# Where a small transpose stands in a step, and three more steps without expert work, in an attention and mixture-of-experts kernel

## Chip, core and metric

The kernel runs on one core of a Trainium2 chip. The metric is the device time of one execution in microseconds. Three executions of the kernel before took 560.89, 562.18 and 559.4 us; their median is 560.89 us.

## What is computed

The input is x with 8 batches of 512 tokens of 128 values, in float32. Each token is normalised (layer norm without weights). The result is x plus an attention block plus a feed-forward block, both fed with the normalised tokens:

```python
xn = _layernorm(x, axis=-1)
x = x + _L0_attn_ref(xn, W1, b1, Wp, bp) + _L0_ffn_ref(xn, gate_w, expert_gate, ...)
...
# attention: 16 heads of 8 dimensions, causal
w = jnp.einsum('bhqd,bhkd->bhqk', q, k) / dk
w = jax.nn.softmax(w * mask - (1.0 - mask) * NEG_BIG, axis=-1)
a = jnp.einsum('bhqk,bhkd->bhqd', w, v)
...
# feed-forward: one shared expert, and the 2 best of 8 routed experts for each token
silu(x @ gw.T) * (x @ uw.T) @ dw.T      # gw, uw: 352x128, dw: 128x352
```

## The kernel before

**Engines and names.** PE is TensorE (matmuls; PEld are its weight loads), DVE is VectorE, ACT is ScalarE, POOL is GpSimd, SP is SyncE, which issues most DMAs. The order of instructions on PE, DVE, ACT and SP is written out by hand: each engine runs its queue in the order in which the Python code issues it. What the code below calls a step is one pass of the inner loop at the end of the function.

**Attention steps.** For each batch there are four groups of four heads, so there are 32 groups (n), and each has five score tiles (i = 0 to 4). That makes 160 steps, step = 5n + i, with a run-in of AHEAD = 9 steps numbered -9 to -1. A step does the following, in this order:

1. `weigh`: PE computes a tile of transposed scores (`fill`, L339) into the PSUM tile scT, which has one buffer, and ACT takes the exponential (L467). The causal mask comes either from extra matmuls (L324) or, from step BUSY = 22 on and as long as not all expert results are placed (`len(placed) < NB`), from POOL (L474).
2. Rows of expert results that are ready are scattered to DRAM by POOL (`to_place`, L679), and row shifts that are ready are written by SP (`puts`, L451).
3. `look(step + 9)`: the softmax needs the maximum of every row before its scores are used. Nine steps ahead PE computes scores in the other orientation (`peak_scores`, L383) into the PSUM tile sc, which also has one buffer, and DVE takes maxima over them (L412, L417, L421, L422). After the fifth tile of a group, `shift_parts` (L427, L432, L433, three small DVE operations) makes the negated maxima, split in two parts.
4. `extra()`: one chunk of expert work, unless the step is in the set `alone`. A chunk (`chunk`) is PE's L664, ACT's tanh (L669) and DVE's L670 and L672. A block of the expert stream has three chunks; along with them come entries for the list `aside`: two `down` groups of the block before (PE's L697, followed by ACT's L704 for a routed block or DVE's L708 for a shared one) and `turn_slots` for a block to come (L638). The stream has 52 blocks: 13 of the shared expert, 36 routed and 3 shared ones at the end. After the last chunk one more call issues the last two `down` groups.
5. `prepare`: ACT copies a mask into the next sc tile (L371) for tiles 0 and 2, once routing is done.
6. `some_routing`: one piece of the routing of tokens to experts, mostly on DVE, up to step 24 (L1042 to L1163).
7. `side`: what is due in this step (the list `ready`), then two entries of `aside`.
8. The weighted sums of earlier tiles (`attend`, L491), and things due `behind` all else (projections L264 and L284, the output projection L579 with its addition to x by DVE, L584). A group pair's sums are turned by L542 (`divide`, three steps after the pair), a batch's by L563 (`turn`).

**The row shift.** The split maxima of a group (128 rows by 32 columns) are transposed by PE (`shift`, L439) into a PSUM tile, DVE copies that to SBUF (L443), and SP writes it as two extra rows of the query operand (`put_shift`, L451), so that the fill adds the negated maximum to each score. In the kernel before, `look` for the fifth tile makes the shift due in the next step, in point 7 of the list above: it is issued behind that step's chunk. That next step is always one with i = 1, step 5n - 4 for group n. SP's two writes are issued at the start of the step after that, and the fills that need them begin at step 5n.

**PSUM buffers.** The tile of the transposed maxima, the chunk's result (gu), the down group's result (y), the turned tokens (s_ps), projections and turned sums all share three rotating PSUM buffers (`misc`). Each new tile takes the buffer of the one issued three places before it and waits until that has been read.

**Steps without expert work.** Steps 3, 5, ..., 19 and 12, 16 and 20 make up the set `alone`, in the stretch in which routing runs. Seven calls come before the run-in and nine in it. The last chunk is issued in step 151 and the last `down` groups in step 152, so steps 153 to 159 have no expert work.

**The end.** When all expert results are in DRAM, POOL adds them to x by 16 gathering DMAs (L732), in the order first places of batches 0 to 5, second places of batches 0 to 5, then first places of batches 6 and 7, then second places of 6 and 7. Those of batches 6 and 7 come after the shared expert's rows for these batches have been added (L708). The last group's sums are then turned and projected, and L584 adds them to x for the last batch. SP and ACT write the output (L1299).

Of the kernel before, what the change touches and what calls it, by code (L numbers as in the profile page):

```python
# [35 lines left out]
AHEAD = 9  # L36
# [17 lines left out]
PIECE = 8  # L54
FILL = 2
BUSY = 22
PLACES = TOPK * NT * P
EPS = 1e-5
MASKED = -1e30
# [8 lines left out]
def attn_moe_kernel(  # L68
# [59 lines left out]
    for i in range(NV):  # L128
        t = const.tile([P, NC, H, 32], F32, name=f"v_ext{i}")
# [71 lines left out]
    for i in range(2):  # L201
        t = const.tile([P, NF, PAIR], F32, name=f"h{i}")
# [17 lines left out]
    table = dram1.tile([NT * P, ROW], F32, name="table")  # L220
    results = dram1.tile([PLACES, E], F32, name="results")

# [71 lines left out]
    def fetch(u, i0=0, i1=HP):  # L294

        from_q, from_k = in_dram[divmod(u, 2)]
        for t in range(2):
            heads = slice(t + 2 * i0, min(t + 2 * i1, HH), 2)
            for a in range(2):
                at_ = SIDE * t + 2 * D * a  # L300
                nc.sync.dma_start(
                    ks[at_ : at_ + 2 * D, u % NU, i0:i1].bitcast(F32),
                    from_k[:, :, heads].rearrange("r d h s -> (r d) h s"),
                )
                if a == 0:
                    nc.sync.dma_start(
                        qs[at_ : at_ + 2 * D, u % NU, i0:i1].bitcast(F32),
                        from_q[:, :, heads].rearrange("r d h s -> (r d) h s"),
                    )
                else:  # L310
                    for r in range(2):
                        nc.sync.dma_start(
                            qs[at_ + D * r : at_ + D * r + D, u % NU, i0:i1].bitcast(F32),
                            from_q[1 - r, :, heads],
                        )
# [92 lines left out]
    def maxima(n, i):  # L408

        ps = peak_scores(n, i)  # L410
        if i == 4:
            nc.vector.tensor_reduce(  # L412
                tops[:, :, :, 2],
                ps.rearrange("p t (u k) -> p t u k", u=2), AX.X, ALU.max,
            )
        elif i in MASKED_TILES:
            nc.vector.tensor_reduce(  # L417
                diag[:, :, i // 2, :], ps.rearrange("p t (b k) -> p t b k", k=P), AX.X, ALU.max
            )
        else:  # L420
            nc.vector.tensor_reduce(tops[:, :, i // 2, 3], ps[:, :, : 3 * P], AX.X, ALU.max)  # L421
            nc.vector.tensor_reduce(tops[:, :, i // 2, 1], ps[:, :, 3 * P :], AX.X, ALU.max)  # L422

    def shift_parts(n):

        top = at.tile([P, 2, 2 * NC], F32, name="row_max")
        nc.vector.tensor_tensor(  # L427
            top.rearrange("p t (i c) -> p t i c", c=NC), tops, diag, ALU.max
        )
        parts = at.tile([P, 2, 2, 2 * NC], F32R, name="m_parts")  # L430
        hi, lo = parts[:, :, 0], parts[:, :, 1]
        nc.vector.tensor_scalar_mul(hi, top, -1.0)  # L432
        nc.vector.scalar_tensor_tensor(lo, top, -1.0, hi.bitcast(F32), ALU.mult, ALU.subtract)  # L433
        return parts
# [28 lines left out]
    def weigh(n, kind, j, by_pool, spare):  # L463

        ps = fill(n, kind, j, by_pool, spare)
        pT = pr.tile([P, 2, S], F32, name="pT")
        nc.scalar.activation(pT, ps, AF.Exp, scale=D**-0.5)  # L467
        if by_pool:
            if kind == "half":
                diagonals = [pT.rearrange("p t (u k) -> p (t u) k", u=2)[:, :, :P]]  # L470
            else:
                diagonals = [pT[:, :, :P]] + ([pT[:, :, 3 * P :]] if kind == "mixed" else [])
            for d in diagonals:
                m = nc.gpsimd.affine_select(  # L474
                    out=d, in_=d, pattern=[[0, d.shape[1]], [1, P]], compare_op=ALU.is_ge,
                    fill=0.0, base=0, channel_multiplier=-1,
                )
                masked.append(m.ins)
        return pT
# [197 lines left out]
    def place_rows(at_, o):  # L677
        with on_pool():
            d = nc.gpsimd.indirect_dma_start(  # L679
                results, bass.IndirectOffsetOnAxis(ap=goal[:, at_ : at_ + 1], axis=0), o, None,  # L680
                bounds_check=PLACES - 1, oob_is_err=False,
            )
# [70 lines left out]
    def due(step, f, to=None):  # L753
        (ready if to is None else to).setdefault(step, []).append(f)

    def look(t):
        n, i = divmod(t, NTILES)
        maxima(n, i)
        if i == NTILES - 1:
            return lambda: due(t - AHEAD + 1, partial(shift, n, shift_parts(n)))  # L760
        return lambda: None

    def side(step, most):

        for f in ready.pop(step, []):
            then(step, f())
        for _ in range(most):
            if aside:
                aside.pop(0)()

    def behind(step):

        for f in behind_all.pop(step, []):
            then(step, f())
# [8 lines left out]
    def extra():  # L783
        do, more = next(beside, (None, []))
        if do is None and not more:
            through.append(True)
        if do is not None:
            do()
        aside.extend(more)
# [129 lines left out]
    def route():  # L919
# [235 lines left out]
        absent = ro.tile([P, NB], F32, name="absent")  # L1155
        nc.vector.tensor_scalar(absent, turn_, 0.5, float(PLACES + S + P), ALU.is_lt, ALU.mult)
        nc.vector.scalar_tensor_tensor(goal, number, -float(P), absent, ALU.add, ALU.add)
# [10 lines left out]
    def some_routing():  # L1168
        if not done_routing and next(routing, "end") == "end":
            done_routing.append(True)  # L1170
            early.close()
            later_pools["wexp"] = pool("wexp", 3 * MB)
            later_pools["inp"] = pool("inp", 6)
            later_pools["turned"] = pool("turned", 3)
            later_pools["scales"] = pool("scales", 4)
# [46 lines left out]
        due(first + (1 if b < 3 else 2), partial(project_qk, b, 1), behind_all)  # L1222
        due(at_ + (8 if b > 1 else 3), partial(project_v, b), behind_all)
    routed = -2
    alone = set(range(3, 21, 2)) | {12, 16, 20}
    for t in range(AHEAD):
        while puts:
            puts.pop(0)()
        parts_then = look(t)
        extra()  # L1230
        parts_then()
        if t - AHEAD >= routed:
            some_routing()
        side(t - AHEAD, 2)
        behind(t - AHEAD)
    for n in range(B * NG):
        b, g = divmod(n, NG)
        waiting = []
        for i, (kind, j) in enumerate(TILES):
            step = n * NTILES + i  # L1240
            if i == 1 and n % 2 == 1 and (n + 3) // 2 < 2 * B:
                fetch((n + 3) // 2)
            by_pool = step >= BUSY and len(placed) < NB
            spare = step >= total_steps - AHEAD + 1 and step % 2 == 1
            waiting.append((kind, j, weigh(n, kind, j, by_pool, spare)))
            while to_place:
                to_place.pop(0)()
            while puts:
                puts.pop(0)()
            parts_then = look(step + AHEAD) if step + AHEAD < total_steps else lambda: None  # L1250
            if step not in alone:
                extra()
            parts_then()
            if done_routing and step + AHEAD + 1 < total_steps:
                prepare(*divmod(step + AHEAD + 1, NTILES))
            if step >= routed:
                some_routing()
            side(step, 2)
            for f in late:
                f()  # L1260
            behind(step)
            late = []
            if i == NTILES - 1 and n == B * NG - 1:
                evacuate(n, av, halves[0])
            if i == 1 and g % 2 == 0:
                av = av_ps.tile([P, S], F32, name="av")
            if i in (1, 4) or (i == 3 and n == B * NG - 1):
                late = [partial(attend, n, waiting, av)]
                waiting = []
            if len(placed) == NB:  # L1270
                for _ in range(2):
                    if to_gather and (to_gather[0][1] < kept or through):
                        gather(*to_gather.pop(0))
        if n == B * NG - 1:
            break
        if g % 2 == 1:
            late.append(partial(evacuate, n, av))
            due(step + 3, partial(divide, n))
        if g == NG - 1:
            due(step + 4, partial(turn, b))  # L1280
            due(step + 5, partial(join, b), behind_all)
# [78 lines left out]
```

## Time and profile before

| What | Value |
|---|---|
| median of three executions | 560.89 us |
| the profiled execution's own time | 561.91 us |
| its span, first to last instruction | 559.9 us |
| mean granted TensorE clock | 0.988 |
| all transposes of maxima (L439) | 32, 0.27 us each, weight load 0.10 |
| their copies by DVE (L443) | 32, 0.27 us each |
| step 0 begins, step 22, step 28 | 52.20, 129.99, 150.50 us |
| step 152 begins, step 153, step 156 | 536.16, 540.02, 543.93 us |

The profile is of one execution. Times are in microseconds from the first instruction. In a line of instructions the columns are start, duration, engine, line, operation, what it writes and reads, sizes and count, and in brackets the idle time of the engine before it with what ended it. Matmuls overlap, and their ends are modelled, so the start of the next instruction says more than a duration. A profile's stretch runs from one given time to another, and shows each engine's busy time in it.

### The profile page before, as it was taken

What the parts mean: (1) busy time and instruction counts of PE and PEld (TensorE: products, weight loads), DVE (VectorE), ACT (ScalarE), POOL (GpSimd) and SP (SyncE); (2) the same over time, 40 slices, a digit from 0 to 9 for tenths busy, and PEclk for the clock granted to TensorE, in tenths of its full rate; (3) what the DMA queues carried; (4) which work ended last, traced back from release to release, by engine and by line L of the source; (5) the groups of instructions that cost most, each with busy time, mean ns of one, the idle gap of its engine ahead of it and who ended that gap; (6) DMA issues with size and microseconds to landing.
All of it is one profiled execution on the core that took longest, in us unless ns stands there. A gap on an engine that the chain in (4) does not pass through costs nothing.

```text
span 559.9 us, 12488 instructions
## 1 busy us (share of the span) xinstructions
PE 530.1 (95%) x4492; PEld 380.5 (68%) x4492; DVE 433.5 (77%) x1057; ACT 353.5 (63%) x566; POOL 260.5 (47%) x439
## 2 busy tenths in 40 slices
PE   4899989889999999999999999999999999999995
PEld 2676655556676777767776777767767777877753
DVE  5878998999877777877787787868688778877731
ACT  4453544564566766877677766867667766777652
POOL 8630020001343556656656556656655766443710
PEclk9999998899999999999999999999999999999997
DMA  6651251816318583584629575674919677640993
GB/s 212 152 75 22 72 83 60 132 51 128 68 39 148 147 156 105 133 207 131 120 87 166 162 165 144 120 167 128 161 45 195 180 164 199 154 110 4 158 207 90
DMA packets 34050, 70.66 MB, mean 126 GB/s; under 512 B 6980, under 2 KB 9288, under 8 KB 33990
## 3 DMA queue, kind: packets, MB, share of 16 engines
q1 hardware_dynamic: 26278, 56.47, 43.8%
q0 software_dynamic: 6848, 13.13, 12.0%
q8 instruction: 36, 0.59, 0.5%
q10 hardware_dynamic: 864, 0.27, 0.2%
q14 instruction: 24, 0.20, 0.2%
HBM read 52.31 MB, written 17.27 MB: 124 GB/s over the span
## 4 chain that ended last, share of the span: by engine, by line
PE 76%; DVE 18%; ACT 2%; issue 2%; DMA 1%; POOL 0%; DVEq 0%; ACTq 0%
PE gu L664 24%; PE av L491 12%; PE y L697 11%; PE scT L339 9%; PE sc L383 9%; DVE diag L417 3%; PE qk_ps L264 3%; DVE tops L421 2%; DVE there L1080 2%; PE p_ps L579 1%; DVE h L672 1%; DVE th L670 1%; PE ot L542 1%; PE s_ps L638 1%; DVE parts L266 1%
## 5 line engine op out<-in xcount | busy, mean ns | idle before, releaser
L467 ACT ACTIVATE pT<-scT 128x1024 f32<-128x1024 f32 x156 | 160.0, 1026 | 63.7 <-PE scT L339 28.1
L474 POOL TENSOR_SCALAR_AFFINE_SELECT pT<-pT 128x256 f32<-128x256 f32 (+1 forms) x173 | 73.7, 440 | 182.3 <-ACT pT L467 179.4
L664 PE MATMUL gu<-sT,w 128*128 128x256 f32 (+1 forms) x480 | 121.2, 379 | 0.3 <-DVE h L672 0.3
L417 DVE TENSOR_REDUCE diag<-sc 128x8 f32<-128x1024 f32 x64 | 78.1, 1221 | 45.9 <-PE sc L383 33.8
L669 ACT ACTIVATE th<-gu 128x256 f32<-128x256 f32 (+1 forms) x156 | 59.6, 382 | 64.8 <-PE gu L664 61.0
L383 PE MATMUL sc<-ks,qs 33*128 33x128 f32 (+3 forms) x896 | 82.0, 283 | 10.0 <-DVE tops L422 4.5
L664 PEld LDWEIGHTS gu<-sT,w 128*128 128x128 f32 x480 | 76.2, 189 | 17.0 <-DVE h L672 0.5
L491 PE MATMUL av<-pT,v_ext 128*32 128x512 f32 (+3 forms) x1024 | 82.6, 440 | 1.8 <-ACT pT L467 1.3
L670 DVE SCALAR_TENSOR_TENSOR th<-th,gu 128x256 f32<-128x256 f32 (+1 forms) x156 | 64.6, 414 | 21.5 <-ACT th L669 18.3
L339 PE MATMUL scT<-qs,ks 35*128 35x512 f32 (+3 forms) x498 | 78.5, 372 | 1.2 <-ACT pT L467 1.2
L679 POOL DMA_INDIRECT results<-o,goal x71 | 72.3, 1018 | 15.8 <-issue 15.8
L383 PEld LDWEIGHTS sc<-ks,qs 33*128 33x128 f32 (+1 forms) x896 | 66.5, 186 | 18.6 <-DVE diag L417 4.9
L623 POOL DMA_INDIRECT s<-table,token x71 | 69.2, 974 | 20.7 <-issue 15.3
L339 PEld LDWEIGHTS scT<-qs,ks 35*128 35x128 f32 x498 | 39.5, 184 | 56.3 <-issue 26.1
L672 DVE TENSOR_TENSOR h<-gu,th 128x256 f32<-128x256 f32 (+1 forms) x156 | 65.6, 421 | 5.4
L421 DVE TENSOR_REDUCE tops<-sc 128x2 f32<-128x768 f32 x64 | 60.8, 950 | 2.5 <-PE sc L383 1.4
L697 PE MATMUL y<-w,h 128*128 128x128 f32 x426 | 59.2, 275 | 0.3 <-DVE parts L266 0.3
L697 PEld LDWEIGHTS y<-w,h 128*128 128x128 f32 x426 | 56.2, 192 | 4.1 <-DVE parts L266 0.7
L371 ACT CAST sc<-mask_q 128x1024 f32<-128x1024 bf16 x50 | 50.9, 1018 | 6.9 <-DVE tops L422 4.8
L664 PE MATMUL gu<-xnT,ws_sb 128*128 128x256 f32 x192 | 54.7, 411 | 0.0
L491 PEld LDWEIGHTS av<-pT,v_ext 128*32 128x32 f32 x1024 | 25.3, 109 | 23.8 <-issue 14.6
L664 PEld LDWEIGHTS gu<-xnT,ws_sb 128*128 128x128 f32 x192 | 33.5, 193 | 10.9 <-issue 3.8
(209 smaller groups left out, 584.3 us busy)
## 6 DMA issues: line engine op xcount, KB each, us to landing
w<-in_w_exp_dram SPq DMA_DIRECT2D x40, 576.0 KB
ks<-dk SPq DMA_DIRECT2D x60, 128.0 KB
dq<-parts SPq DMA_DIRECT2D x16, 256.0 KB
dk<-parts SPq DMA_DIRECT2D x16, 256.0 KB
qs<-dq SPq DMA_DIRECT2D x64, 64.0 KB
x_sb<-results POOLq DMA_DIRECT2D x16, 256.0 KB
qs<-dq SPq DMA_DIRECT2D x30, 128.0 KB
table<-rows SPq DMA_DIRECT2D x4, 520.0 KB
```

The costliest lines, as they stand in the source:

```text
L339: nc.tensor.matmul(out_, lhsT=k[:, ts(i, P)], rhs=q[:, i * P :], start=first, stop=True, skip_group_check=True,)
L383: nc.tensor.matmul(ps[:, jj % 2, ts(at_, P) if count == 1 else ds(at_ * P, count * P)], lhsT=q[:, ts(c, P)], rhs=k[:, key * P : (key + cou ...
L417: nc.vector.tensor_reduce(diag[:, :, i // 2, :], ps.rearrange("p t (b k) -> p t b k", k=P), AX.X, ALU.max)
L421: nc.vector.tensor_reduce(tops[:, :, i // 2, 3], ps[:, :, : 3 * P], AX.X, ALU.max)
L467: nc.scalar.activation(pT, ps, AF.Exp, scale=D**-0.5)
L474: m = nc.gpsimd.affine_select(out=d, in_=d, pattern=[[0, d.shape[1]], [1, P]], compare_op=ALU.is_ge, fill=0.0, base=0, channel_multiplier=-1,)
L491: nc.tensor.matmul(av[32 * jj : 32 * jj + 32, c * P :], lhsT=v_ext[b % NV][:, c, at_, :], rhs=weights, start=(c == 0 and g % 2 == 0), stop ...
L664: nc.tensor.matmul(gu[:, i, part], lhsT=w[c][:, ds(i * FP + f * P, P)], rhs=sT[:, part], start=True, stop=True,)
L670: nc.vector.scalar_tensor_tensor(th, th, 1.0, gu[:, 0], ALU.add, ALU.mult)
L672: nc.vector.tensor_tensor(h[own_, f, :slots], gu[own_, 1], th[own_], ALU.mult)
L679: d = nc.gpsimd.indirect_dma_start(results, bass.IndirectOffsetOnAxis(ap=goal[:, at_ : at_ + 1], axis=0), o, None, bounds_check=PLACES - 1 ...
L697: nc.tensor.matmul(y, lhsT=h[:, f, ts(c, P)], rhs=w[c % len(w)][:, ds(2 * FP + f * P, P)], start=(f == 0), stop=(f == NF - 1),)
```

## The change

There are two edits. First, a transposed shift is no longer put into the list of things due in the next step, but into a list of its own, `shifts`. That list is emptied in the next step right behind the scores and ahead of the chunk from step SOON = 25 on, and behind the chunk, but ahead of `prepare` and routing, before that. Second, steps 22, 24 and 26 join the set `alone`, so they issue no chunk. The number of chunks stays the same; the calls that these steps would have made are made by later ones.

```diff
+SOON = 25
...
+    shifts = []
+
+    def turn_shifts(when):
+        while shifts and when:
+            shifts.pop(0)()
+
     def look(t):
         n, i = divmod(t, NTILES)
         maxima(n, i)
         if i == NTILES - 1:
-            return lambda: due(t - AHEAD + 1, partial(shift, n, shift_parts(n)))
+            return lambda: shifts.append(partial(shift, n, shift_parts(n)))
         return lambda: None
...
-    alone = set(range(3, 21, 2)) | {12, 16, 20}
+    alone = set(range(3, 21, 2)) | {12, 16, 20, 22, 24, 26}
     for t in range(AHEAD):
         while puts:
             puts.pop(0)()
         parts_then = look(t)
         extra()
+        turn_shifts(True)
         parts_then()
...
             parts_then = look(step + AHEAD) if step + AHEAD < total_steps else lambda: None
+            turn_shifts(step >= SOON)
             if step not in alone:
                 extra()
+            turn_shifts(step < SOON)
             parts_then()
```

## The prediction

> **What bounds the kernel now.** I read the page first, then the waits of PE, then each engine's timeline. I number a step by its transposed-score fill (L339), which opens it on PE; there are 160, and the first starts at 52.20 us.
>
> ```profile
> PE 530.1 (95%) x4492; PEld 380.5 (68%) x4492; DVE 433.5 (77%) x1057; ACT 353.5 (63%) x566; POOL 260.5 (47%) x439
> ...
> PEclk9999998899999999999999999999999999999997
> ```
>
> PE is busy nearly everywhere. The clock is short of full in two early slices and in the last one. The waits of PE say how little idle time there is to win:
>
> ```profile
> PE sc L383 <- DVE tops L422: 4.5, 7, 1.2
> PE sc L383 <- DVE diag L417: 3.1, 4, 1.4
> ...
> PE gu L664 <- DVE h L672: 0.3, 1, 0.3
> ```
>
> Columns: total us, times, longest. Scores (L383) wait for DVE's maxima, because the score tile has one PSUM buffer. In the timeline nearly all of these waits lie before step 22, where routing loads DVE. Only one expert matmul group (L664) ever waits, for 0.3 us. After step 27 the steps are PE back to back, so a step costs what its matmuls cost. The six steps that the change strips and their neighbours (22 to 27), a stretch each:
>
> ```profile
> 129.99:133.20 3.21, 3.21 (x25) 1.92 (x24) 2.93 (x10) 1.41 (x2) 0.77 (x2) 1.00 0.20 69
> 133.20:136.70 3.50, 3.50 (x34) 2.79 (x31) 3.33 (x10) 1.97 (x3) 0.77 (x2) 1.00 0.75 130
> 136.70:140.00 3.30, 3.30 (x27) 2.94 (x26) 3.16 (x11) 1.43 (x3) 0.64 (x1) 1.00 0.90 124
> 140.00:143.17 3.17, 3.17 (x36) 1.81 (x35) 3.03 (x11) 1.41 (x2) 0.41 (x1) 1.00 0.55 62
> 143.17:147.06 3.89, 2.93 (x26) 2.23 (x23) 3.02 (x8) 2.35 (x3) 0.92 (x2) 1.00 0.01 1
> 147.06:150.50 3.44, 3.44 (x27) 2.24 (x26) 3.21 (x9) 2.39 (x3) 2.48 (x4) 1.00 0.20 44
> ```
>
> Columns: length, then busy us of PE, PEld, DVE, ACT, POOL, then clock. PE is full except for 0.96 us in step 26, but DVE is nearly full too: 18.68 of 20.51 us. So work taken off PE here soon meets DVE.
>
> **Prices.** Step 12 goes from scores (93.04) to weighted sums (94.06) over the L542 turns in 1.02 us; step 22 has a chunk between and takes from 130.34 to 132.21, 1.87. One chunk costs PE 0.85. Steps 134 and 139 differ by the six matmuls of L697, 2.43 against 1.76: 0.67. On DVE a chunk is two operations, start to start 0.45 and 0.40, and each L697 group one of 0.28.
>
> **Part 1, transposes from step 25 on.** Nothing is added: 26 transposes (L439), their DVE copies (L443) and two small DMAs each move forward within their step. Step 26 has no chunk to pass, so 25 really move. The transpose issues in 0.11 us (161.37 to 161.48) before or after the chunk alike. It needs the split maxima of L433, which end 0.4 to 1.8 us before the chunk starts (381.12 against 381.54 in the tightest, step 101), so PE should not wait there; if it did, the chunk and all PE work would queue behind it. DVE's copy, 0.27, now goes between the diagonal maxima and the tanh product. In step 136 the maxima end at 493.17 and ACT's tanh at 493.35, so 0.18 of the copy fills a hole. On SP the writes stay where they are, popped at the next step's start; they are only ready some 1 us sooner. They were issued at 495.0 for a fill at 500.94, so no fill gains. One true gain: the three small PSUM buffers rotate, and the next step's chunk now reuses the buffer that the copy frees, not the one that L672 frees. That removes the single 0.26 us wait (step 37). Before step 25 the move passes only routing and prepared masks: same DVE sum, nothing. Bounds for part 1: -0.5 (twice the visible wait) to +1.3 (25 times 0.05, half an issue slot); I take -0.26, the row itself.
>
> **Part 2, the stripped steps.** The three missing calls delay all later expert work by three calls, exactly one block of three chunks. The pattern of chunk against step, period three, is thus unchanged. By step 28, 3 chunks and 2 down groups have left PE: 3 x 0.85 + 2 x 0.67 = 3.9 us. I walk the queues by the rows:
> - Step 22: 2.36 instead of 3.21. DVE ends its maxima at 132.12, then does routing (1.24), divide (0.8), and starts step 23's maxima at 134.1, before at 135.12.
> - Steps 23 and 24 shrink to 2.83 and 1.78 on PE, which reaches step 25 at about 137.0. DVE still owes a chunk (0.85), routing of L1147 to L1153 (1.2) and step 24's maxima (1.2), ending near 138.5. Step 25's scores wait there about 1.4 us.
> - Step 26: the scores wait 0.2 for ACT's mask copy and go at 142.4 (before 144.63). Step 27: PE waits 0.5 for maxima that end at 144.3; its scores go at 144.4, before at 147.40.
>
> Gain at step 28: about 2.9, since some 2 us of new waits replace the old 0.96. It is carried to the end. A second gain: the last routed result is placed three steps later, so steps 145 to 147 keep POOL's masks and drop PE's (L324). Steps 146 and 126 have equal matmuls but for these, 2.86 against 2.67; three such steps give about 0.5.
>
> **What comes back.** The same 3.9 us return in steps 152 to 155, where there were two down groups at 152 and then no expert work. What can swallow them is this idle time:
>
> ```profile
> 541.94 0.50 PE L339 MATMUL sc<-qs,ks 35*128 35x512 f32 x2 [0.65 <-ACT pT L467]
> ...
> 545.74 1.07 PE L491 MATMUL av<-pT,v_ext 128*32 128x512 f32 x8 [0.65 <-ACT pT L467]
> ...
> 548.66 1.07 PE L491 MATMUL av<-pT,v_ext 128*32 128x384 f32 x16 [0.65 <-ACT pT L467]
> ```
>
> Only the first wait (step 155) has the returned chunks before it; it goes. The others follow fills without expert work and stay. Against it, the last down groups need the last chunk's hidden tile. In step 151 that tile ended 3.0 us after the step's start (534.35 to 537.37), ACT's exponential going first. Step 154 is only about 1.5 us long, so step 155 waits about 0.6 for it; before, the turns of L542 covered most of this. Returned: 3.9 - 0.65 + 0.6 - 0.24 (the old wait of step 152) = 3.6.
>
> **Sum.** -2.9 - 0.5 - 0.26 + 3.6 = -0.1 us on a profiled time of 561.91 (span 559.9 and 2.0 around it). The profiled run is 1.0 above the median, 560.89, so I forecast 560.8.
>
> **The clock.** This view of four stretches shows a price that the sum leaves out:
>
> ```profile
> 82.24:85.65 3.41, 2.52 (x30) 1.76 (x29) 3.36 (x9) 1.67 (x3) 0.21 (x1) 1.00 0.00 0
> 85.65:89.07 3.42, 3.42 (x14) 2.44 (x17) 2.33 (x7) 0.81 (x2) 0.00 (x0) 0.50 0.00 0
> 95.89:99.31 3.42, 2.05 (x29) 1.20 (x25) 3.38 (x11) 2.70 (x3) 0.00 (x0) 1.00 1.01 345
> 99.31:102.72 3.41, 3.41 (x14) 2.37 (x14) 3.38 (x14) 1.04 (x2) 0.00 (x0) 0.50 1.07 132
> ```
>
> Twice a stretch in which PE ran almost only score matmuls of 33 to 64 rows, 2.0 to 2.5 us of them, was followed by 3.41 us at half clock. Step 10 took 5.79 us there, against 3.84 for its like (step 45). [...] By the rows a busy but thin stretch is enough, and the sum would be +1.6. I follow the rows, as a rival.
>
> **Rivals.**
> 1. *DVE keeps up* (0.20). If routing's small operations overlap more than I walk, the 2 us of waits vanish: -0.1 - 2.0 = -2.1, 558.8; with the 0.6 of step 155 gone too, 558.2. For it: DVE has only 18.68 of 20.51 us. Against: DVE ran without a gap over 0.2 us from 130.65 to 144.8, and its order is fixed.
> 2. *Slower: the clock halves in steps 24 to 28* (0.17). Between step 25's weighted sums (to 142.0) and step 27's chunk (144.8) PE has 2.8 us of thin work, where 81.5 to 85.41 tripped it. It decides if a clock window of 3.41 us falls onto this gap with under about 0.5 us of full-height matmuls in it. Price 1.7 each: 562.5, and twice, 564.2.
> 3. *The last gather ends last* (0.08). The last expert row update moves from 539.42 to about 542.8, and POOL's last gathers hang on it:
>
> ```profile
> 539.75 1.76 POOL L732 DMA_DIRECT2D x_sb<-results  x2 [7.22 <-DMA x_sb<-results]
> 547.32 0.87 POOL L732 DMA_DIRECT2D x_sb<-results  x1 [5.81 <-DMA x_sb<-results]
> ```
>
> SP saw that last one landed at 551.58; the final addition (L584) starts at 555.69. A slack of 4.1 against a delay of 3.4 leaves 0.7. Slower transfers by 2 us would give +1.3, 562.1.
>
> **Chances.** Forecast 0.55, rivals 0.20, 0.17, 0.08. A measurement tells about 0.5%, 2.8 us. Over that faster takes the longer half of rival 1 and a little beyond: 0.15. Over that slower takes most of rival 2 doubled, or with 3: 0.18. Within: 0.67. The range takes in rival 1's 558.2 and rival 2's 564.2.
>
> **What would show it.** Right: scores of step 25 waiting over 1 us for L422; step 26's wait for the mask copy shrinking to 0.2; step 28 near 147.6 and step 152 near 532.5; L664 with no wait on L672; no L324 in steps 145 to 147; step 156 within 0.5 us of 543.93. Wrong: no wait at step 25 (rival 1), clock 0.50 between 135 and 150 (rival 2), L584 waiting for the gather (rival 3), or transposes that wait for L433.

## The result and the profile after

The changed kernel took 566.11 us (median of 6 runs, 564.53 to 569.33), the kernel before, on the same chip, 561.16 us (6 runs, 559.4 to 562.18). The ratio is 1.0089, with a 95% interval of 1.0068 to 1.0110: slower by 5.0 us, where -0.1 was forecast, and above the range. The profiled execution of the changed kernel took 564.53 us, with a span of 562.3, against 561.91 and 559.9.

From here on a line number of the changed kernel is one higher than before, up to the edited loop (L339 is L340, L664 is L665, L732 is L733). The page after:

```profile
PE 528.7 (94%) x4476; PEld 380.2 (68%) x4476; DVE 434.1 (77%) x1057; ACT 353.9 (63%) x566; POOL 262.2 (47%) x443
...
PEclk9999999999899999999999999999999999999997
```

Next to the page of before nothing stands out: the busy times differ by 1.7 us or less, and the clock row has one 8 where it had two. The change has to be read stage by stage. I cut both profiled executions at the same steps:

| Stretch | before, us | after, us | difference |
|---|---|---|---|
| up to step 22 | 129.99 | 128.12 | -1.87 |
| steps 22 to 27 | 20.52 | 21.40 | +0.88 |
| steps 28 to 151 | 385.65 | 383.07 | -2.57 |
| steps 152 to 155 | 7.77 | 11.95 | +4.18 |
| step 156 to the end | 15.96 | 17.74 | +1.78 |

Most of the first row isn't the change: step 10 took 5.79 us before, under the half clock that starts at 85.65, and 4.18 after, where the profiled execution had none. The stripped steps, a stretch for each of 22 to 27, with the columns as in the prediction (the last two are the busy share of the DMA engines and GB/s):

```profile
128.12:130.42 2.30, 2.30 (x22) 1.16 (x22) 2.23 (x8) 1.02 (x1) 0.66 (x2) 1.00 0.33 108
130.42:133.24 2.82, 2.82 (x28) 2.07 (x25) 2.68 (x8) 1.35 (x2) 0.88 (x3) 1.00 0.83 150
133.24:135.21 1.97, 1.97 (x18) 1.56 (x17) 1.83 (x8) 1.58 (x3) 0.27 (x1) 1.00 0.76 111
135.21:142.49 7.28, 5.70 (x41) 3.54 (x40) 6.06 (x18) 2.42 (x3) 0.78 (x2) 0.77 0.42 54
142.49:144.19 1.70, 1.12 (x15) 0.81 (x11) 0.69 (x1) 1.02 (x1) 0.00 (x0) 1.00 0.00 0
144.19:149.51 5.32, 5.23 (x26) 3.46 (x26) 3.13 (x7) 2.32 (x3) 1.18 (x3) 0.68 0.01 3
```

Steps 22 to 24 and 26 shrink about as walked. Steps 25 and 27 swell from 3.17 to 7.28 and from 3.44 to 5.32. The new waits and the clock (0.77 and 0.68) share this: in the kernel with FIRST = 12 below, at full clock, the same two steps take 5.67 and 3.76. The same time cut into stretches of 3.41 us at the clock's own changes:

```profile
134.90:138.32 3.42, 1.84 (x13) 1.26 (x12) 3.25 (x13) 1.02 (x1) 1.06 (x2) 1.00 0.76 106
138.32:141.73 3.41, 3.41 (x17) 2.13 (x19) 3.09 (x8) 1.40 (x2) 0.00 (x0) 0.50 0.24 25
141.73:145.15 3.42, 2.75 (x39) 1.74 (x31) 1.41 (x2) 1.44 (x2) 0.41 (x1) 1.00 0.00 0
145.15:148.56 3.41, 3.41 (x18) 2.74 (x17) 2.05 (x4) 1.82 (x3) 0.77 (x2) 0.50 0.02 5
```

The halved stretches are the second and the fourth; each follows a window in which PE was busy 1.84 or 2.75 of 3.41 us. The new wait lies in the first of these windows. PE's timeline in step 25 (start, duration, instruction, idle time before it):

```profile
135.21 0.50 PE L340 MATMUL scT<-qs,ks 35*128 35x512 f32 x2
137.28 0.50 PE L384 MATMUL sc<-ks,qs 33*128 33x256 f32 x4 [1.58 <-DVE tops L423]
137.72 1.53 PE L665 MATMUL gu<-xnT,ws_sb 128*128 128x256 f32 x4
```

The wait is the forecast one (1.4 forecast, 1.58 measured), and the chunk behind it takes 1.53 instead of 1.13 at the lower clock.

The four steps in which the work comes back, first of the kernel before, then of the changed one:

```profile
536.16:543.93 7.77, 7.09 (x90) 4.46 (x90) 2.42 (x8) 4.18 (x5) 1.76 (x2) 1.00 0.77 196
```

```profile
532.59:544.53 11.94, 11.75 (x114) 8.23 (x114) 5.10 (x15) 5.48 (x8) 3.98 (x5) 1.00 1.12 213
```

PE's busy time grows by 4.66 and its idle time falls from 0.68 to 0.19. Last, the end. POOL's timeline holds the last scatter of routed results and the gathers, DVE's the final addition. First the kernel before (its last gather is in the prediction), then the changed one:

```profile
515.46 1.00 POOL L679 DMA_INDIRECT results<-o,goal  x1 [0.16 <-issue]
518.35 6.38 POOL L732 DMA_DIRECT2D x_sb<-results  x7 [1.90 <-DMA results<-o,goal]
```

```profile
555.69 0.42 DVE L584 TENSOR_TENSOR x_sb<-p_ps,x_sb 128x256 f32<-128x256 f32 x1 [2.53 <-PE p_ps L579]
556.54 0.42 DVE L584 TENSOR_TENSOR x_sb<-p_ps,x_sb 128x256 f32<-128x256 f32 x1 [0.43 <-PE p_ps L579]
```

```profile
521.62 1.00 POOL L680 DMA_INDIRECT results<-o,goal  x1 [0.15 <-issue]
524.52 7.28 POOL L733 DMA_DIRECT2D x_sb<-results  x8 [1.90 <-DMA results<-o,goal]
...
546.81 1.76 POOL L733 DMA_DIRECT2D x_sb<-results  x2 [9.00 <-DMA x_sb<-results]
554.52 0.87 POOL L733 DMA_DIRECT2D x_sb<-results  x1 [5.95 <-DMA x_sb<-results]
```

```profile
558.55 0.76 DVE L585 TENSOR_TENSOR x_sb<-p_ps,x_sb 128x256 f32<-128x256 f32 x2 [4.80 <-DMA x_sb<-results]
```

Before, the addition waited for p_ps, PE's output projection of the last batch; now it waits for the last gather. PE began p_ps at 554.77 (554.43 before), and before, the addition came 1.26 after that. So it could have come at about 556.0 and comes 2.5 later. The kernel's end is delayed by less: before, the second half of the addition waited another 0.43 for p_ps, and now both halves run together. From the start of p_ps to the end it is 7.50 instead of 5.46, so the late gather costs 2.0 in this execution.

### The profile page after: what moved, and what is told of

It is laid out like the page before. It is cut to its first block, busy times and chain, and to the rows that moved or that the text cites. A ratio compares the mean times of both kernels' runs of the same rounds, so it can differ in the third digit from the quotient of the medians.

```text
span 562.3 us, 12458 instructions
## 1 busy us (share of the span) xinstructions
PE 528.7 (94%) x4476; PEld 380.2 (68%) x4476; DVE 434.1 (77%) x1057; ACT 353.9 (63%) x566; POOL 262.2 (47%) x443
## 4 chain that ended last, share of the span: by engine, by line
PE 70%; DVE 18%; issue 5%; DMA 3%; POOL 2%; ACT 2%; DVEq 0%; POOLq 0%; ACTq 0%
PE gu L665 22%; PE y L698 11%; PE av L492 11%; PE scT L340 9%; PE sc L384 8%; DVE diag L418 3%; PE qk_ps L265 3%; DMA x_sb<-results 2%; DVE tops L422 2%; DVE there L1087 2%; POOL x_sb L733 1%; PE s_ps L639 1%; DVE th L671 1%; DVE parts L267 1%; DVE stats L828 1%
## 5 line engine op out<-in xcount | busy, mean ns | idle before, releaser
L475 POOL TENSOR_SCALAR_AFFINE_SELECT pT<-pT 128x256 f32<-128x256 f32 (+1 forms) x177 | 75.3, 440 | 187.6 <-ACT pT L468 184.1
L665 PE MATMUL gu<-sT,w 128*128 128x256 f32 (+1 forms) x480 | 119.1, 375 | 0.0
L665 PEld LDWEIGHTS gu<-sT,w 128*128 128x128 f32 x480 | 76.5, 190 | 15.1
L340 PE MATMUL scT<-qs,ks 35*128 35x512 f32 (+3 forms) x498 | 78.4, 372 | 2.0 <-ACT pT L468 1.8
L340 PEld LDWEIGHTS scT<-qs,ks 35*128 35x128 f32 x498 | 39.5, 184 | 57.6 <-issue 21.1
L665 PE MATMUL gu<-xnT,ws_sb 128*128 128x256 f32 x192 | 55.2, 413 | 0.6 <-DVE v_ext L290 0.6
L665 PEld LDWEIGHTS gu<-xnT,ws_sb 128*128 128x128 f32 x192 | 33.8, 195 | 11.4 <-issue 4.0
```

Source lines behind the costliest of these rows:

```text
L340: nc.tensor.matmul(out_, lhsT=k[:, ts(i, P)], rhs=q[:, i * P :], start=first, stop=True, skip_group_check=True,)
L475: m = nc.gpsimd.affine_select(out=d, in_=d, pattern=[[0, d.shape[1]], [1, P]], compare_op=ALU.is_ge, fill=0.0, base=0, channel_multiplier=-1,)
L665: nc.tensor.matmul(gu[:, i, part], lhsT=w[c][:, ds(i * FP + f * P, P)], rhs=sT[:, part], start=True, stop=True,)
```

## Experiments

**Theory.** Three things: the transposes gain some 2 us; two halved clock windows in steps 25 to 28, next to the new wait, cost some 3 (3.8 in the expectations, 3.2 measured); and the chain of gathers starts at the last routed result, is delayed with it, and ends last. **Rivals**: the transposes cost something that the stages hide; the chain hangs on the last expert row, as I had taken it; the stripping costs the same wherever it stands, so the clock isn't the point. A ratio is always to the kernel before on the same chip, because chips differ: the kernel before took 556.0, 556.5 and 561.5 us on the three that were used here.

**First edit alone** (with `shifts` and `turn_shifts`, and the old set; the lines are against the changed kernel).

```diff
-    alone = set(range(3, 21, 2)) | {12, 16, 20, 22, 24, 26}
+    alone = set(range(3, 21, 2)) | {12, 16, 20}
```

> Only the first edit: shifts transposed ahead of the chunk from step 25 on, and the old set of steps without expert work. Theory 1 (three terms: the moved transpose saves 0.09 us of PE in each of some 22 to 25 steps, two halvings of the clock in steps 25 to 28 cost some 3.8, the chain of gathers ends 2.8 later than the projection): about -2.2 us against before, 559.0, clock 1.00 from 110 us to the end of the expert work. Rival (the prediction's own reading, the move is worth 0.26): 560.9, no difference that can be measured.

Measured: 553.19 us, ratio 0.9952 (0.9933 to 0.9971). Steps 22 to 27 take 20.40, and the final addition waits for PE again:

```profile
547.49 0.87 DVE L585 TENSOR_TENSOR x_sb<-p_ps,x_sb 128x256 f32<-128x256 f32 x2 [1.76 <-PE p_ps L580]
```

This half of the change makes the kernel faster, by 2.7 us. So the rival that the transposes cost something falls.

**Second edit alone.**

```diff
-    alone = set(range(3, 21, 2)) | {12, 16, 20}
+    alone = set(range(3, 21, 2)) | {12, 16, 20, 22, 24, 26}
```

> Only the second edit: steps 22, 24 and 26 without a chunk, the shift where it was. Theory 1: all of the loss and none of the gain of the first edit, so about 2.2 slower than the changed kernel, 568.3, with halved clock between 135 and 150 us and the last addition waiting for the last gather. Rival (the moved transpose itself causes part of the loss, for instance by waiting for the split maxima): clearly faster than the changed kernel, below 565.

Measured: 564.2 us, ratio 1.0156 (1.0132 to 1.0180). The clock is at half from 138.13 to 144.95 and from 148.37 to 151.78, steps 22 to 27 take 22.69, and the final addition waits 4.87 for the gather. All of the loss is in this edit, and more than all. It is also more than the 2.2 us beyond the changed kernel that were expected: 0.7 to 0.8% of the whole time, some 4 us, with a third halved window.

**One shared block later** (the changed kernel with one shared block fewer ahead of the routed ones, so that the routed results are placed earlier).

```diff
-FIRST = 13
+FIRST = 12
```

> The changed kernel with 12 instead of 13 shared blocks ahead of the routed ones and 4 instead of 3 behind them: the routed blocks come one block (three calls) earlier, so the last routed result is placed in the step where it was before the change. Same work in sum. Theory 1: the gathers end before the projection again, the last addition no longer waits, 2.8 less than the changed kernel, about 563.3, with the clock still halved in steps 25 to 28. Rival (the clock explains the whole loss and the gathers only follow it): no difference to the changed kernel, 566.

Measured: 556.89 us, ratio 1.0014 (0.9985 to 1.0042). The steps 22 to 27 as one stretch, POOL's gathers and the final addition of this kernel:

```profile
129.63:147.85 18.22, 15.98 (x138) 10.51 (x137) 16.60 (x46) 9.73 (x12) 5.95 (x11) 1.00 0.43 71
```

```profile
506.80 1.00 POOL L680 DMA_INDIRECT results<-o,goal  x1 [0.16 <-issue]
...
538.61 0.86 POOL L733 DMA_DIRECT2D x_sb<-results  x1 [6.04 <-DVE x_sb L709]
543.05 0.86 POOL L733 DMA_DIRECT2D x_sb<-results  x1 [3.58 <-DMA x_sb<-results]
```

```profile
550.34 0.87 DVE L585 TENSOR_TENSOR x_sb<-p_ps,x_sb 128x256 f32<-128x256 f32 x2 [1.76 <-PE p_ps L580]
```

Two readings. The last result is placed at 506.80, 20.6 us ahead of step 152, as in the kernel before (20.7), where the changed kernel has 11.0; steps 152 to 155 take as long as in the changed kernel (11.95). The final addition waits for PE again. So the place of the last routed result decides whether the gather ends last, not the last expert row. The row does hold back one gather here (released by L709), but only because the chain is early enough to meet it. And without being aimed at, this profile has no half clock in steps 22 to 28, against the expectation (its halved windows begin at 97.05 and 120.94), and steps 22 to 27 take 18.22 at full clock. So the lower time is not the gather's alone. It isn't settled how often this kernel escapes: its twelve runs took 553.85 to 561.20 us at mean clocks of 0.994 down to 0.978, and only one was profiled.

**Keeping PE busy in the thin stretch** (the changed kernel, with matmuls repeated into the same tile: the output projection of batch 0, in step 24, three times, and the transpose of step 26 nine times; the values stay the same).

```diff
-        nc.tensor.transpose(
+        for _ in range(9 if n == 6 else 1):
+            nc.tensor.transpose(
...
-        for c in range(n):
+        for c in list(range(n)) * (3 if b == 0 else 1):
```

> The changed kernel with extra full-height matmuls in the thin stretch: the output projection of the first batch (step 24) is computed three times and the transpose of step 26 nine times, into the same tiles, with the same results. It adds some 2 us of PE work there, mostly inside waits. Theory 1: the clock stays at 1.00 between 130 and 150 us, and the time falls by 3.8 less what of the added work is not hidden (up to 1), to about 563, in all terms but the gathers. Rival (the halved clock costs nothing, DVE being the bound there): no gain, or up to 2 slower, 566 to 568.

Measured: 557.97 us, ratio 1.0035 (1.0018 to 1.0052). Steps 22 to 27, and the final addition:

```profile
129.81:148.01 18.20, 18.20 (x162) 13.04 (x162) 16.47 (x46) 9.73 (x12) 3.76 (x9) 1.00 0.42 72
```

```profile
551.99 0.76 DVE L586 TENSOR_TENSOR x_sb<-p_ps,x_sb 128x256 f32<-128x256 f32 x2 [4.54 <-DMA x_sb<-results]
```

With the added matmuls PE is busy throughout at full clock, and the stretch is 3.2 us shorter than in the changed kernel (21.40). The extra work only fills what were waits: the kernel with FIRST = 12 takes the same 18.2 without it. So the halved clock costs 3.2 there, and the rival that it costs nothing falls. That the filling is what kept the clock up rests on two profiles, this one and the one with both remedies. The gather still ends last, as it should by the theory.

**Three other steps stripped** (the kernel before, steps 100, 102 and 104 without a chunk, far from routing).

```diff
-    alone = set(range(3, 21, 2)) | {12, 16, 20}
+    alone = set(range(3, 21, 2)) | {12, 16, 20, 100, 102, 104}
```

> The kernel before (old shift), with steps 100, 102 and 104 freed of expert work, where PE is dense and routing long done, in place of 22, 24 and 26. The stream is late by three calls all the same, so the last routed result is placed three steps later, without the thin stretch. Theory 1: the clock stays at 1.00 there, and the loss is the gather chain's alone: it starts some 6 to 9 us later and ends 2 to 5 behind the projection, so 2 to 5 slower than before, the last addition waiting for the last gather. Rival (only the thin stretch costs): no difference to before.

Measured: 562.09 us against 556.51, ratio 1.0114 (1.0091 to 1.0136), 5.6 us where 2 to 5 were expected. Steps 22 to 27 take 20.51, as before. The last routed result is placed at 517.98, 10.9 us ahead of step 152, and the final addition waits for the gather:

```profile
555.66 0.76 DVE L584 TENSOR_TENSOR x_sb<-p_ps,x_sb 128x256 f32<-128x256 f32 x2 [4.57 <-DMA x_sb<-results]
```

Beside the profile of the kernel before on that chip (below), steps 99 to 106 take 2.1 less, steps 152 to 155 5.2 more and the end 2.7 more. So the return and the late gather are costs of delaying the expert stream here too, without a thin stretch. This also limits the clock's part: the edit loses without it. Stripping 22, 24 and 26 instead cost 1.56%, against 1.14% here, on two chips and with intervals that just touch; that the place matters is told by the profiles (22.69 us against 20.51 for steps 22 to 27, although the former have three chunks less) rather than by the times.

**Both remedies** (FIRST = 12 and the repeated matmuls in the changed kernel; the diffs are those above).

> Both remedies at once: 12 shared blocks ahead of the routed ones, and the repeated projection (step 24) and transpose (step 26). Theory 1: no halved clock between 130 and 150 us and no wait for the last gather, so what is left of the change is the gain of the moved transpose (2 to 3) and new waits of about 1: 0 to 3 us faster than before, some 3 faster than with the earlier routed blocks alone. Rival (the two remedies remove one and the same loss): no faster than the better one of them alone.

Measured: 556.22 us, ratio 0.9998 (0.9984 to 1.0012). Steps 22 to 27 take 18.21 and the final addition waits for PE. With both costs gone the kernel equals the one before. It does not reach the first edit alone: the 2.3 us that the stripped steps gain are less than the 4.2 that come back in steps 152 to 155. The 3 us beyond FIRST = 12 alone that were expected did not show: the intervals 0.9984 to 1.0012 and 0.9985 to 1.0042 overlap, so by whole times the rival that both remedies remove one loss is not excluded. The profiles tell them apart: with the repeated matmuls alone the final addition still waits for the gather, and with FIRST = 12 it does not.

**The changed kernel and the kernel before again, on the chip of the last two comparisons.**

> The changed kernel itself, on the chip of this comparison. All theories: about 0.9% slower than before, by 3 to 6 us, of which theory 1 puts 2 to 3 on the last gather and the rest on halved clock in steps 25 to 28, less 2 to 3 for the moved transpose.

> The kernel before itself, for a profile on the chip of this comparison: step times in the middle that can be set beside those of the others without a difference between chips. Theory 1: 0.09 us more in each step with a shift than in the kernels with the first edit, and equal other steps; the rival has no difference in them.

Measured: the changed kernel 560.33 us against 556.51, ratio 1.0074 (1.0049 to 1.0098); the kernel before, a single run, 557.87. By stretches the two profiles differ by -2.7 up to step 22 (more halved clock in the kernel before), +0.9 in steps 22 to 27 (two halved windows again, from 138.80 and 145.63), -3.7 in 28 to 151, +4.2 in 152 to 155 and +4.6 behind, where the final addition waits for the gather in the one and for p_ps in the other. The twelve runs of the changed kernel have mean clocks of 0.973 to 0.989 and times of 556.8 to 564.3; the 23 of the kernel before 0.988 to 0.994 and 555.0 to 558.2. The run with 0.973 is the longest, and the two with 0.989 take 556.8 and 559.5: how much is halved varies from run to run.

**Why the moved transpose gains.** The time of a step with i = 1 fell by 0.09 us in nearly all of them. Step 116, PE's timeline, in the kernel before and after:

```profile
428.43 0.56 PE L383 MATMUL sc<-ks,qs 33*128 33x128 f32 x8
428.92 1.13 PE L664 MATMUL gu<-sT,w 128*128 128x256 f32 x4
429.88 0.27 PE L439 MATMUL mT_ps<-ident,m_parts 128*32 128x128 f32 x1
429.99 0.83 PE L697 MATMUL y<-w,h 128*128 128x128 f32 x6
```

```profile
426.18 0.56 PE L384 MATMUL sc<-ks,qs 33*128 33x128 f32 x8
426.67 0.28 PE L440 MATMUL mT_ps<-ident,m_parts 128*32 128x128 f32 x1
426.79 1.03 PE L665 MATMUL gu<-sT,w 128*128 128x256 f32 x4
427.66 0.83 PE L698 MATMUL y<-w,h 128*128 128x128 f32 x6
```

The same instructions take 1.56 us from the first score matmul to y before, and 1.48 after. In both, 0.20 us after the last score matmul's start a weight load is recorded, and the matmul is recorded 2 to 3 ns behind it. If that first load is exposed, it is the chunk's before (128 columns, 186 ns) and the transpose's after (32 columns, 95 ns), while the chunk's own load then lies beside the transpose. To test that, the transposes were widened to 128 columns, the 32 of the split maxima and 96 of zeros, once behind the scores and once in the old place, with the first edit alone beside them. The main lines:

```diff
-        parts = at.tile([P, 2, 2, 2 * NC], F32R, name="m_parts")
+        parts = wide[n % 2][:, :32].rearrange("p (t r m) -> p t r m", t=2, r=2)
...
-        return parts
+        return wide[n % 2]
...
-        ps = misc([32, P], "mT_ps")
+        ps = misc([P, P], "mT_ps")
...
-        nc.vector.tensor_copy(mT, ps)
+        nc.vector.tensor_copy(mT, ps[:32])
```

> The first edit alone (transposes behind the scores from step 25, old set of stripped steps), but each transpose takes 128 columns instead of 32: the split maxima and 96 columns of zeros. Its weight load is then as long as the chunk's, about 190 ns instead of 95; the copy still reads 32 rows. Theory (behind the scores the first weight load is exposed, and the edit gains because a load of 95 ns takes the place of one of 186): the 0.09 us a step goes, steps such as 116 and 121 take 2.67 us again instead of 2.58, and the kernel takes about 2.2 us more than the first edit alone, ratio to before about 1.000. Rival (the gain is in the order itself, in the buffers or on DVE): steps 116 and 121 stay at 2.58, ratio about 0.995.

> The kernel before with the same wide transposes in their old place, behind the chunk. Theory: the load of 190 ns lies beside the chunk's last matmul (0.21 us to the next start), so it costs nothing: steps 116 and 121 stay within 0.03 us of 2.67, ratio 1.000. Rival (a wide load costs its 0.09 us wherever it stands): steps 116 and 121 at 2.76, 2.3 us more in all, ratio 1.004.

> The first edit alone once more, as the measure for the wide one on the same chip. Theory: steps 116 and 121 at 2.58, ratio 0.995 to 0.997, that is 1.7 to 2.8 us faster than before. Rival (the first measurement was the luck of one chip's clock windows): ratio 0.999 or more.

Measured, against 561.54 us: wide behind the scores 558.8, ratio 0.9950 (0.9928 to 0.9971); wide in the old place 561.18, 0.9991 (0.9972 to 1.0011); the first edit again 558.56, 0.9943 (0.9919 to 0.9968). So the gain of the first edit repeats. The whole times don't tell the wide transpose from the narrow one behind the scores: 0.9950 is what the rival expected, and the 1.1 us by which the two should differ (25 times 0.045) are within the intervals. The steps tell them apart, and there neither expectation was met: they lie halfway. Step 116 takes 2.67 before, 2.58 with the first edit, 2.62 with the wide transposes behind the scores, 2.67 with them in the old place; over all steps with i = 1 the median differences to before are -0.090, -0.044 and 0.000. The reason for the half is in the groups of this tile by form, first of the kernel before, then of the wide one behind the scores (shortest, median and longest, ns):

```profile
L439 PEld LDWEIGHTS mT_ps<-ident,m_parts x32: 94/97/99, 43.7 to 535.7; 128*32 128x32 f32 x32
```

```profile
L444 PEld LDWEIGHTS mT_ps<-ident,wide x32: 137/139/142, 42.3 to 533.7; 128*128 128x128 f32 x32
```

I had expected 190 ns; the wide load takes 139. The saving follows the load: 186 - 95 = 91 ns for 0.090 us, and 186 - 139 = 47 ns for 0.044. In the old place, beside the chunk's last matmul, the longer load costs nothing (2.67 us for step 116 with either load). That carries the theory, with the size of the wide load mis-set in the expectation; had the order alone made the gain, the wide transposes behind the scores would have kept all of it.

A load's size is not the whole of its time: two loads of 128 columns by 128 rows took 139 and 186 ns here, against 95 for 32 columns by 128 rows. What else counts stays open.

**The best version** is the first edit alone: 0.9952 and 0.9943 on two chips.

## Why the prediction was wrong, point by point

**Steps 22 to 27, the walk: right in kind.** The scores of step 25 waited 1.58 for L423 (1.4 forecast). The scores of step 26 didn't wait for ACT's mask copy (0.2 forecast), and step 27 waited 0.59, for ACT's exponential and not for maxima (0.5 forecast). At full clock the six steps take 18.2 instead of 20.5, a gain of 2.3; forecast 2.9.

**"The clock": the price left out of the sum, and the failed step.** Rival 2 had the mechanism and about the price (1.7 each; step 10 shows 1.6, with 5.79 us against 4.18 at full clock, and the two windows of the changed kernel 3.2), and I gave it 0.17 because it seemed to need luck. It had the place of one of the two windows, from 141.73; the other, from 134.90, holds the new wait of step 25 itself. Its condition was too narrow: by the starts in PE's timeline these windows hold about 0.9 and 1.0 us of matmuls over all 128 rows, not under 0.5 (an estimate: in the kernel before, the stretches from 82.24 and 95.89, each followed by half clock, hold 0.47 and 0.07). The halving came twice in both profiles of the changed kernel, and over three windows with the second edit alone; of the four profiles that have this thin stretch unfilled, only the one with FIRST = 12 escaped. With repeated matmuls the 3.2 us were gone. What made it seem rare was that one window of 3.41 us had to fall right. But in the profiles of before and after the halved stretches lie on one grid of their own length, 3.413 us: the changed kernel's begin at 97.36, 138.32 and 145.15, 12 and 14 such lengths behind the first (40.96 and 47.79 us), and those of the kernel before at 85.65 and 99.31, 4 lengths apart (13.65 us between the recorded starts). PE's longest idle gap in steps 22 to 27 of the changed kernel was 1.58 us. At full clock steps 25 and 26 take 7.4 us (with FIRST = 12), over two windows of such a grid, so at least one whole window lies inside at any phase. That made a halving likely enough to belong into the sum, but not certain: with FIRST = 12 the windows from 138.01 and 141.42, with PE busy 2.62 and 2.75, weren't followed by half clock.

**"The last gather ends last": the second failed step.** I hung the gathers on the last expert row (539.42 to 542.8, a delay of 3.4 against a slack of 4.1). The chain starts at the last routed result: the first gather is issued 2.9 us after it, the last one 28.6 to 30.0 us after the first (518.35 to 547.32 before, 524.52 to 554.52 after, 511.28 to 539.83 in the first edit alone), and the final addition can start 4.0 us behind that. The result came 6.2 later (515.46 to 521.62), because the stream is three steps late, some 8 us (an estimate, three steps of about 2.7), and the earlier gain takes back only part. With 1.0 more in the chain itself the delay is 7.2. The slack was 4.4 (547.32 + 4.0 against 555.69), and PE's own path ends 0.3 later: the addition comes 2.5 late, as seen, and the end 2.0. The price varies: on the other chip the same stretch behind step 156 took 4.6 more.

**Part 1: outside its own bounds.** I took -0.26, with a bound of -0.5. The single wait of L664 for L672 did go (step 37 from 4.38 to 4.05). But I compared only the issue slot of the transpose, 0.11 us in both places, and not which weight load is left exposed at the switch from scores to other work. That is 25 times 0.09, 2.2 us; with step 37, 2.5; measured over the whole kernel, 2.7 and 3.2.

**What comes back: 4.2, forecast 3.6.** Step 152 began at 532.59, as forecast (532.5), but by luck: the profile of before had lost 1.9 early, and the clock's 3.2 stood against gains that weren't in the sum. Step 155 waited 0.19 for the last hidden tile (0.6). The mis-sized term is the 3.9: in these steps PE's busy time grew by 4.66. The price of 0.85 was from step 22; the chunk of step 154 takes 1.06 from its start to the next scores.

**The masks** (L324) are gone from steps 145 to 147, which take 1.6 us less; their other matmuls changed as well, and steps 140 to 144 take 0.9 more (the same on the other chip), so the 0.5 was not measured by itself.

**The sum, with what the runs showed:** -2.3 + 3.2 (clock) - 2.6 (steps 28 to 151: transposes, step 37, masks, with the 0.9 against them) + 4.2 + 2.0 (gather) = +4.5. The difference of the medians is 5.0; the rest is less than the spread of the runs. The spans of the two profiled executions differ by only 2.4, as the one before had lost 1.9 more before step 22, and took 10.50 instead of 10.24 from step 156 to p_ps, where its half clock began 1.5 us earlier. Not settled are some tenths of a us in steps 28 to 151, where single steps (96, 126) vary from run to run.

## What to carry to other kernels

When work is delayed, follow every serial transfer chain from its first issue, not only from its last release: a chain of nearly fixed length (28.6 to 30.0 us here) moves with its start, and its slack is used up first. Where a busy TensorE becomes thin for longer than two of the 3.41 us stretches seen here, put the halved clock into the sum and not among the unlikely rivals, since a whole one lies inside at any phase; here it came in three of four profiles. Where the order of matmul groups can be chosen, try the group with the shortest weight load behind the switch; here that was worth 0.09 us each time, and the kernel needed nothing else for it.

## What the runs showed of the hardware that was not expected

- In the changed kernel the clock was halved after windows in which PE was busy 1.84 to 2.75 of 3.41 us, with no idle gap over 1.58. It wasn't halved after others in the same kernel with as little (the window from 117.84, 2.17; from 124.66, 2.41), while with FIRST = 12 the window from 117.53, busy 2.18, was followed by half clock. Busy time alone doesn't decide; what does was not found. No run here separates matmuls over few rows from few matmuls.
- Behind the switch from the scores, what the first weight load was shorter by came back in the time of the step: loads of 95, 139 and 186 ns went with gains of 0.090, 0.044 and 0 us.
- Gathers with addition held each other up here: POOL issued the four behind the first eight 1.2 to 1.3 us apart, each released by the landing of an earlier one (532.21, 533.55, 534.81, 536.05 after; 526.93, 528.23, 529.50, 530.77 before).
- Chips differ by 1% for the same kernel: the kernel before took 556.0, 556.5 and 561.5 us on three of them, with mean clocks of 0.986 to 0.997, 0.988 to 0.994 and 0.983 to 0.997.
